# Adding x to the projected attention on TensorE with an identity product

## The chip, the cores and the metric

The kernel runs on one core of one Trainium2 chip. The metric is device time in microseconds, of the median of several executions. Engines are named TensorE (PE; its weight loads are PEld), VectorE (DVE), ScalarE (ACT), GpSimd (POOL) and SyncE (SP).

## The reference

The input x has shape (8, 384, 64, 64), in float32. Two layers are applied, each as x plus a function of the group-normed x. The first is a channel attention, the second a selective scan over four directions. All convolutions of 1x1 are matrix products over the channels.

```python
# layer 0: channel attention
q = _dwconv3x3(_conv1x1(x, wq), dwq)      # k and v likewise
q, k, v = (split(q), split(k), split(v))  # 8 heads of 48 channels
q = _l2norm(q)
k = _l2norm(k)
attn = softmax(einsum('bhcn,bhdn->bhcd', q, k) * temperature)
out = einsum('bhcd,bhdn->bhcn', attn, v)
out = _conv1x1(out, wproj)
...
x = x + _L0_conv_ref(_gn(x), ...)
x = x + _L1_conv_ref(_gn(x), ...)         # its group norm needs statistics of the new x
```

## The kernel before, in words

The eight images are worked on one after the other. Each goes through `channel_attention` and then through `selective_scan`. Channels lie on partitions, in three tiles of 128 (index m or j); pixels lie along the free dimension, 4096 per image, in eight chunks of 512 (index c). Everything is float32. The image x stays in SBUF from its load until the scan has used it.

`channel_attention` makes k, then q, then v with the same helper `conv` (L203 to L244). For a tile m and a stretch of rows y0 to y1, TensorE makes the 1x1 convolution in chunks of eight image rows (L219, into a PSUM tile "pc"), ScalarE copies each chunk out with its bias into the SBUF tile "pre" (L224) and starts the depthwise sum with the centre tap (L228), and VectorE adds the other eight taps (L240). The tile "pre" has two buffers.

The last part of the attention makes v and projects it. The product of the attention matrix and the projection has been folded into one matrix mT (L337, L340). The rows come in three stretches, 0 to 32, 32 to 48 and 48 to 64 (L359), each for the three tiles m. Where a stretch ends, its last row of pre-activation is kept (L367, "edge") and put in front of the next stretch's "pre" (L213), so that x itself is not needed there again.

`project_out(m, c)` (L346 to L356) handles one block of 128 channels by 512 pixels. TensorE makes three products over the three tiles of v into one PSUM tile (L349). VectorE adds it to x in place (L354) and takes the statistics for the next group norm from the result (L355). SP stores the new x to DRAM (L356), where the finish step of the following image's attention reads it.

Blocks are queued in `todo` as their rows of v become known, and are issued after later convolutions, six at a time and only for m above 0 (L368 to L370). A stretch of 32 rows gives twelve blocks, a stretch of 16 gives six. So 18 of an image's 24 blocks are issued inside the loop, in three groups of six: after the conv of tile 1 and of tile 2 in the stretch 32 to 48, and after that of tile 1 in the stretch 48 to 64. The last six are issued after the loop (L374).

The PSUM tiles of `conv` and of `project_out` come from one pool, `ps_c`, under one tag with three buffers (L168), so a block and a conv chunk wait for each other's buffers.

From the second image on, the loop also carries the finish of the image before (L371, `finish_part`, L856 to L878): SP loads a part of the scan's result and of the stored x, ScalarE normalizes it (L865), TensorE turns it (L872), ScalarE applies the gelu (L873), VectorE adds x (L877) and SP stores it. Two parts follow each convolution.

In this part the order of the instructions on each engine is chosen by a scheduler that works from priorities and estimated durations when the program is built; nothing in it is pinned. Each engine then works through its queue in that order. In the scan, by contrast, the order is written out by hand (`pin`), and the change doesn't touch it. After the attention, the scan starts with the group norm's factors (L114 to L140) and normalizes x in place (L417, L422).

Of the kernel before, what the change touches and what calls it, by code (L numbers as in the profile page):

```python
# [17 lines left out]
NJ = C // P  # L18
H = W = 64
L = H * W  # L20
CH = 512
# [53 lines left out]
def tile_channel_attention_then_selective_scan(ctx: ExitStack, tc: tile.TileContext, a: dict):  # L75
    nc = tc.nc
# [7 lines left out]
    ident = const.tile([P, P], F32, name="ident")  # L84
# [13 lines left out]
    for name in ("dt_bias", "Ds", "ln_w", "ln_b", "temp"):  # L98
        t = const.tile(list(a[name].shape), F32, name=name)
# [43 lines left out]
    def load_x(b):  # L143

        xs = []
        for j in range(NJ):
            t = big.tile([P, L], F32, tag="x", bufs=NJ, name=f"x{b}_{j}")
            for h in range(2):
                nc.sync.dma_start(t[:, bass.ts(h, L // 2)], x_d[b, j, :, bass.ts(h, L // 2)])
            xs.append(t)  # L150
        stats = big.tile([P, NJ, NCH, nc.vector.BN_STATS_DIM], F32, tag="st0", name=f"st0{b}")
        return xs, stats
# [6 lines left out]
    def channel_attention(b, x, stats, before):  # L159
# [5 lines left out]
        with ExitStack() as st:  # L165
# [122 lines left out]
            for m in range(NJ):  # L288
# [7 lines left out]
                for t4 in range(NT // 4):  # L296
                    qT = work.tile([P, 4, P], F32, tag="qT", name=f"qT{b}{m}_{t4}")
                    to_tokens(acc, t4, qT, f"q{b}{m}")
                    for i in range(4):
                        t = 4 * t4 + i  # L300
                        nc.tensor.matmul(
                            pa[:, :wd], lhsT=qT[:, i, :], rhs=kT[:, t, lo:hi],
                            start=t == 0, stop=t == NT - 1,
# [18 lines left out]
            if before is not None:  # L322
                scale, shift = token_norm(b, wp, work, before[2])

                def emit(i):
                    t = work.tile([P, L], F32, tag="acc", name=f"fin{b}_{i}")
                    room = [t[:, n * FT * NJ : (n + 1) * FT * NJ] for n in range(3)]
                    finish_part(*before, i, scale, shift, room, ps_t, "pt")
# [3 lines left out]
            for j in range(NJ):  # L332
                pm = ps_a.tile([P, CH], F32, tag="pa", name=f"pmt{b}{j}")
                src = [i for i in range(NJ) if _overlaps(i, j)]
                for i in src:
                    nc.tensor.matmul(
                        pm[:, :C], lhsT=attn[:, i, bass.ts(j, P)], rhs=wj[:, i, :],  # L337
                        start=i == src[0], stop=i == src[-1],
# [4 lines left out]
            x1_d = dram.tile([NJ, P, L], F32, tag="x1d", bufs=2, name=f"x1d{b}")  # L343
            stats1 = big.tile([P, NJ, NCH, nc.vector.BN_STATS_DIM], F32, tag="st1", name=f"st1{b}")

            def project_out(m, c):  # L346
                pc = ps_c.tile([P, CH], F32, tag="pc", name=f"pp{b}{m}_{c}")
                for j in range(NJ):
                    nc.tensor.matmul(  # L349
                        pc, lhsT=mT[:, j, bass.ts(m, P)], rhs=v[:, j, bass.ts(c, CH)],  # L350
                        start=j == 0, stop=j == NJ - 1,
                    )
                s = x[m][:, bass.ts(c, CH)]
                nc.vector.tensor_add(s, s, pc)  # L354
                nc.vector.bn_stats(stats1[:, m, c, :], s)  # L355
                nc.sync.dma_start(x1_d[m, :, bass.ts(c, CH)], s)  # L356


# [1 line left out]
            todo, left, edges = [], list(range(L // FT)) if emit else [], {}  # L360
            for y0, y1 in zip(parts, parts[1:]):
                for m in range(NJ):
                    pre = conv("v", wv, bv, m, y0, y1, v[:, m, y0 * W : y1 * W], edges.get(m))
                    if y1 < H:
                        edges[m] = work.tile([P, W], F32, tag="edge", bufs=4, name=f"edge{b}{m}_{y1}")
                        o = (y1 - 1 - max(0, y0 - 1)) * W
                        nc.scalar.copy(edges[m], pre[:, o : o + W])  # L367
                    if m > 0:  # L368
                        for _ in range(min(len(todo), 6)):
                            project_out(*todo.pop(0))  # L370
                    for _ in range(min(len(left), 2)):  # L371
                        emit(left.pop(0))
                todo += [(m, c) for c in range(y0 * W // CH, y1 * W // CH) for m in range(NJ)]
            for t in todo:  # L374
                project_out(*t)
        return x, x1_d, stats1

    def selective_scan(b, x1, stats1):
# [514 lines left out]
    x, before = load_x(0), None  # L893
    x_stats(*x, [(j, c) for j in range(NJ) for c in range(NCH)])
    for b in range(B):
        x1, x1_d, stats1 = channel_attention(b, *x, before)
        y_d, x = selective_scan(b, x1, stats1)
        before = (b, x1_d, y_d)
# [50 lines left out]
```

## Time and profile before

| | us |
|---|---|
| median of 3 runs | 20936.09 (20930.49 to 20946.7) |
| the profiled execution | 20922.88 |
| its span, first to last instruction | 20921.1 |
| VectorE busy / TensorE busy | 19312.5 / 19277.1 |
| ScalarE busy / GpSimd busy | 18022.9 / 15437.3 |
| products of `project_out` (L349), 1152 records | 556.1 |
| adds of x (L354), 192 | 129.7, one 687 ns |
| statistics of the new x (L355), 192 | 130.9, one 694 ns |
| mean granted TensorE clock | 0.966 of full speed |

The span is slightly shorter than the time of the same execution, since the time also holds what lies around the first and the last instruction. A line such as L349 is the number of the line in the kernel. "out<-in" names the tile that an instruction writes and those that it reads. In a timeline the first two columns are the start and the length of a merged run of instructions, "x36" says how many there are, and the bracket at the end gives how long the engine stood idle before and who ended that. A table of stretches has, for each stretch, its length and then the busy time of each engine with the count of instructions, the granted TensorE clock, the busy share of the DMA engines and GB/s.

### The profile page before, as it was taken

Reading aid. Unit: us, or ns where it says so; the run is one execution under the profiler, and the core shown is the slowest. Engines: PE = TensorE matmul, PEld = TensorE weight load, DVE = VectorE, ACT = ScalarE, POOL = GpSimd, SP = SyncE. Lnnn points to the kernel's source line nnn. Section 1 sums busy time; section 2 is a strip of 40 time slices with the busy share of each in tenths; the row PEclk is TensorE's granted clock in tenths of the full one; section 3 lists DMA queues with packets and bytes.
Section 4 is the critical chain, followed back from the end, with each engine's and each line's share of the span. In section 5 each row is a group of like instructions: output and inputs, shape, how many; then the busy total and the mean of one; then the engine's idle time right before and its main releaser. Section 6 shows DMA issues by size and latency. Waiting matters only on the chain. (4 is left out here: it accounts for less than half of the span.)

```text
span 20921.1 us, 319325 instructions
## 1 busy us (share of the span) xinstructions
PE 19277.1 (92%) x118256; PEld 10697.2 (51%) x118256; DVE 19312.5 (92%) x17310; ACT 18022.9 (86%) x32267; POOL 15437.3 (74%) x6918
## 2 busy tenths in 40 slices
PE   7999989999899998999989999899998999989998
PEld 4555445555455554555445555455544555445554
DVE  8999989999899988999889998899988999889998
ACT  3999949999599985999859998599985999859998
POOL 0999809998199981999719997199971999729997
PEclk8999989999899998999989999899998999989999
DMA  1222322223223232222322223223232232322223
GB/s 41 78 91 93 95 75 81 91 92 96 73 81 91 92 99 70 81 91 92 102 69 81 91 92 102 70 79 91 93 99 71 81 92 92 97 71 82 91 91 116
DMA packets 953163, 1807.95 MB, mean 86 GB/s; under 512 B 125904, under 2 KB 646352, under 8 KB 945456
## 3 DMA queue, kind: packets, MB, share of 16 engines
q1 hardware_dynamic: 950736, 1787.40, 27.0%
q8 instruction: 932, 15.27, 0.3%
q14 instruction: 631, 5.17, 0.1%
q10 hardware_dynamic: 864, 0.12, 0.0%
HBM read 1468.39 MB, written 318.77 MB: 85 GB/s over the span
## 5 line engine op out<-in xcount | busy, mean ns | idle before, releaser
L553 POOL TENSOR_TENSOR db<-w,B 128x1536 f32<-128x1536 f32 x4088 | 14134.1, 3464 | 639.9 <-DVE h L565 283.9
L565 DVE TENSOR_TENSOR_SCAN h<-da,ca,db 128x512 f32<-128x512 f32 x10752 | 13085.7, 1268 | 627.2 <-ACT da L544 316.6
L599 ACT ACTIVATE hc<-pt,ct 128x384 f32<-128x384 f32 x15128 | 8517.5, 579 | 452.1 <-PE pt L587 353.0
L544 ACT ACTIVATE da<-dt,neg_a 128x512 f32<-128x512 f32 x12288 | 8508.7, 696 | 183.3 <-DVE h L565 148.2
L587 PE MATMUL pt<-ident,h 128*128 128x128 f32 x49152 | 8097.9, 288 | 582.9 <-ACT hc L599 412.3
L587 PEld LDWEIGHTS pt<-ident,h 128*128 128x128 f32 x49152 | 5150.5, 141 | 5243.1 <-ACT hc L599 2648.5
L622 PE MATMUL py<-hc,pair 128*64 128x384 f32 x24576 | 5347.7, 514 | 9.2 <-DVE ys L673 9.2
L402 POOL MEMSET wdt<- 128x1536 f32 x8 | 11.0, 1378 | 3614.3 <-DMA x1d<-x 3614.3
L628 PE MATMUL py<-hc,pair 128*64 128x128 f32 x24576 | 2114.2, 281 | 0.0
L565 DVE TENSOR_TENSOR_SCAN h<-da,db 128x512 f32<-128x512 f32 x1536 | 1814.0, 1232 | 160.6 <-ACT da L544 98.9
L622 PEld LDWEIGHTS py<-hc,pair 128*64 128x64 f32 x24576 | 1218.5, 135 | 1020.3 <-issue 950.9
L628 PEld LDWEIGHTS py<-hc,pair 128*64 128x64 f32 x24576 | 1568.5, 137 | 208.9 <-issue 130.4
L451 PE MATMUL px<-x,wx 128*44 128x128 f32 x6144 | 1482.4, 339 | 35.3 <-ACT x L417 29.1
L451 PEld LDWEIGHTS px<-x,wx 128*44 128x44 f32 x6144 | 649.1, 122 | 816.7 <-issue 750.9
L528 POOL TENSOR_TENSOR w<-x,dt 128x512 f32<-128x512 f32 x744 | 1056.0, 1419 | 0.0
L579 POOL COPY ca<-h 128x6 f32<-128x6 f32 x1792 | 339.3, 189 | 943.7 <-DVE h L565 940.4
L510 PE MATMUL pd<-xd,wdt 128*128 128x512 f32 x1536 | 781.5, 618 | 73.0 <-ACT hc L599 60.6
L601 DVE TENSOR_SCALAR hc<-pt,ct 128x384 f32<-128x384 f32 x1256 | 736.2, 603 | 54.8 <-PE pt L587 25.4
L349 PE MATMUL pp<-v,mT 128*128 128x512 f32 x1152 | 556.1, 637 | 121.8 <-DVE v L240 57.3
L520 ACT ACTIVATE dt<-pd,dt_bias 128x512 f32<-128x512 f32 x768 | 474.6, 685 | 21.3 <-PE pd L510 17.7
L510 PEld LDWEIGHTS pd<-xd,wdt 128*128 128x128 f32 x1536 | 274.6, 192 | 387.0 <-issue 187.1
L349 PEld LDWEIGHTS pp<-v,mT 128*128 128x128 f32 x1152 | 229.5, 205 | 402.0 <-issue 314.4
(315 smaller groups left out, 11723.8 us busy)
## 6 DMA issues: line engine op xcount, KB each, us to landing
B<-bcd SPq DMA_DIRECT2D x2048, 512.0 KB
yd<-ys SPq DMA_DIRECT2D x128, 576.0 KB
ys<-yd SPq DMA_DIRECT2D x256, 288.0 KB
yd<-ys SPq DMA_DIRECT2D x256, 288.0 KB
x<-in_x SPq DMA_DIRECT2D x48, 1024.0 KB
x1d<-x SPq DMA_DIRECT2D x192, 256.0 KB
fy<-yd SPq DMA_DIRECT2D x128, 384.0 KB
fin<-yd SPq DMA_DIRECT2D x112, 384.0 KB
```

The lines of the kernel that those rows point to most:

```text
L349: nc.tensor.matmul(pc, lhsT=mT[:, j, bass.ts(m, P)], rhs=v[:, j, bass.ts(c, CH)], start=j == 0, stop=j == NJ - 1,)
L451: pin(nc.tensor.matmul(split(pxs[s][:XR, :])[:, part, :], lhsT=wx[:, j, k, :], rhs=view(x1[j], k, c)[:, part, :], start=i == 0, stop=i == ...
L510: pin(nc.tensor.matmul(pds[j], lhsT=wdt[:, k, bass.ts(j, P)], rhs=xds[s], start=True, stop=True))
L528: pin(eng.tensor_mul(split(ws[s][:, j, :]), view(x1[j], k, c), split(dts[s][:, j, :])))
L544: pin(nc.scalar.activation(t, dts[s][:, j, :], AF.Exp, scale=neg_a[:, j, k, n : n + 1]))
L553: pin(eng.tensor_mul(t, ws[g // NP], bts[g][:, v : v + 1, :].broadcast_to([P, NJ, CH])))
L565: pin(nc.vector.tensor_tensor_scan(h, da, db, 0.0 if start else carries[s - 1][:, j, n : n + 1], ALU.mult, ALU.add,))
L587: pin(nc.tensor.transpose(t[:, bass.ts(j, P)], h2s[g][:, j, bass.ts(q, HP), :].rearrange("p l v -> p (l v)"), ident))
L599: pin(eng.activation(out, src, AF.Copy, scale=scale))
L601: pin(eng.tensor_scalar_mul(out, src, scale))
L622: pin(nc.tensor.matmul(py[f * HP : (f + 1) * HP, lb, :C], lhsT=pair, rhs=hc[:, f, :], **flags))
L628: pin(nc.tensor.matmul(py[f * HP : (f + 1) * HP, j, C:], lhsT=pair, rhs=hc[:, f, bass.ts(j, P)], **flags,))
```

## The change

For the 18 blocks that are issued inside the loop, `project_out` now begins the PSUM sum with a product of the identity matrix and the chunk of x, so that the finished PSUM tile holds the new x. VectorE takes the statistics from PSUM; it no longer adds. ScalarE copies the tile from PSUM over the chunk of x, and the store follows that copy. For the six blocks after the loop the code is as before. The identity matrix `ident` was in SBUF already.

```diff
-            def project_out(m, c):
+            def project_out(m, c, end):
+
+                s = x[m][:, bass.ts(c, CH)]
                 pc = ps_c.tile([P, CH], F32, tag="pc", name=f"pp{b}{m}_{c}")
+                if not end:
+                    nc.tensor.matmul(pc, lhsT=ident, rhs=s, start=True, stop=False)
                 for j in range(NJ):
                     nc.tensor.matmul(
                         pc, lhsT=mT[:, j, bass.ts(m, P)], rhs=v[:, j, bass.ts(c, CH)],
-                        start=j == 0, stop=j == NJ - 1,
+                        start=end and j == 0, stop=j == NJ - 1,
                     )
-                s = x[m][:, bass.ts(c, CH)]
-                nc.vector.tensor_add(s, s, pc)
-                nc.vector.bn_stats(stats1[:, m, c, :], s)
+                if end:
+                    nc.vector.tensor_add(s, s, pc)
+                    nc.vector.bn_stats(stats1[:, m, c, :], s)
+                else:
+                    nc.vector.bn_stats(stats1[:, m, c, :], pc)
+                    nc.scalar.copy(s, pc)
                 nc.sync.dma_start(x1_d[m, :, bass.ts(c, CH)], s)
...
                         for _ in range(min(len(todo), 6)):
-                            project_out(*todo.pop(0))
+                            project_out(*todo.pop(0), False)
...
             for t in todo:
-                project_out(*t)
+                project_out(*t, True)
```

In the built program of the changed kernel the scheduler has also moved a few neighbours on TensorE: the transposes of a finish part (L872), of which the first used to stand before the last block of a group, stand after it. On ScalarE the copies stand between the finish activations. The wait that is written into each copy is for VectorE, whose statistics read the same PSUM tile.

## The prediction

> **What bounds the kernel now.** I started with the page's busy times, to see that no one engine rules everything.
>
> ```profile
> PE 19277.1 (92%) x118256; PEld 10697.2 (51%) x118256; DVE 19312.5 (92%) x17310; ACT 18022.9 (86%) x32267; POOL 15437.3 (74%) x6918
> L349 PE MATMUL pp<-v,mT 128*128 128x512 f32 x1152 | 556.1, 637 | 121.8 <-DVE v L240 57.3 <-ACT pre0v L224 15.5 <-DVE x L354 9.0
> ```
>
> TensorE and VectorE tie at 92%, over 2,100 us of scan per image that the change doesn't touch. The row L349 counts 1152 records for 8 images x 24 blocks x 3 products = 576 products, so a fp32 product is two records ("passes"). What the change is worth is read where these blocks run: the last 110 us of each attention. I asked for the busy time in five stretches of the second image (2890 us to 3062 us).
>
> ```profile
> core 0: us, PE busy (x) PEld busy (x) DVE busy (x) ACT busy (x) POOL busy (x), PEclk, DMA share, GB/s
> 2955.00:2982.00 27.00, 26.91 (x70) 12.57 (x71) 23.77 (x29) 10.60 (x21) 0.00 (x0) 0.91 0.56 183
> 2982.00:3004.40 22.40, 22.40 (x62) 10.44 (x61) 18.50 (x22) 8.44 (x15) 0.00 (x0) 1.00 0.52 177
> 3004.40:3036.40 32.00, 30.25 (x85) 13.31 (x84) 29.79 (x32) 16.18 (x27) 0.00 (x0) 1.00 0.53 181
> 3036.40:3062.00 25.60, 17.31 (x41) 7.77 (x40) 19.39 (x23) 0.00 (x0) 1.83 (x3) 0.80 0.28 93
> ```
>
> Call the first three A, B, C; each holds one group of six blocks of the 18 that change. In A and B TensorE is busy throughout and VectorE is not; in C both nearly are. The fourth is the tail, whose blocks keep their code. The same stretches of images 2 and 7 have the same figures within 0.3 us. Then the timeline, VectorE and TensorE, for who waits.
>
> ```profile
> 2981.90 1.27 DVE L240 SCALAR_TENSOR_TENSOR v<-pre1v,dwv,v 128x1008 f32<-128x1008 f32 x1 [3.23 <-ACT v L228]
> 3004.43 7.74 DVE L240 SCALAR_TENSOR_TENSOR v<-pre1v,dwv,v 128x1008 f32<-128x1008 f32 x6 [3.54 <-ACT v L228]
> 3017.77 0.68 DVE L354 TENSOR_TENSOR x<-x,pp 128x512 f32<-128x512 f32 x1
> 3036.41 10.23 DVE L240 SCALAR_TENSOR_TENSOR v<-pre1v,dwv,v 128x1008 f32<-128x1008 f32 x8 [1.59 <-ACT v L228]
> ```
>
> ```profile
> 2954.77 15.70 PE L349 MATMUL pp<-v,mT 128*128 128x512 f32 x30 [5.94 <-ACT pre1v L224]
> 2980.32 15.67 PE L349 MATMUL pp<-v,mT 128*128 128x512 f32 x36
> 3018.50 2.84 PE L349 MATMUL pp<-v,mT 128*128 128x512 f32 x6 [0.66 <-DVE x L354]
> 3029.05 5.42 PE L219 MATMUL pc1v<-x,wv 128*128 128x512 f32 x12 [0.38 <-DVE x L354]
> ```
>
> ```profile
> 3002.53 0.69 ACT L224 ACTIVATE pre1v<-pc1v,bias1v 128x512 f32<-128x512 f32 x1 [1.89 <-PE pc1v L219]
> 3003.25 1.15 ACT L228 ACTIVATE v<-pre1v,dwv 128x1024 f32<-128x1024 f32 x1
> ```
>
> At the end of each group VectorE stands still until ScalarE's L228, which waits for L224, which waits for the conv product L219, which stands behind the group's products in TensorE's queue. So the chain through A and B is: 36 passes of L349, the next conv's passes, L224, L228, first tap. VectorE has 3.23 and 3.54 us to spare.
>
> [...] Here a pass goes every 0.43 us (36 passes in 15.67 us), a product in 0.86: the trace decides. [...] after 5.94 us of idle the weight loads of A's first passes stand 0.86 us apart. [...] no row of before has two readers of a block, but the built order shows each copy waiting for VectorE, so statistics and copy of a block are in series. [...] the trace has 687 for the add.
>
> **The change, part by part.** 18 blocks x 8 images = 144 changed blocks.
>
> Removed: 144 adds on VectorE. One lasts 687 ns, but neighbours overlap: in the timeline the next instruction starts 0.60 us after an add. 6 x 0.60 = 3.6 us a group, 86 us in all. In A and B VectorE is not on the chain, so this only lengthens its idle time; in C part of it counts.
>
> Statistics from PSUM: before reads SBUF in 694 ns. [...] the add that reads PSUM takes 687[...]; I take 0. VectorE's slack covers it[...].
>
> Added: 144 identity products, two passes of 0.4275 us each: 0.86 x 6 = 5.1 us a group, 123 us in all. Their weight loads lie beside passes (PEld is half busy). In the built order the identity product stands first in each block. Could it fill the 5.94 us ahead of A? Those wait for PSUM: all three buffers hold the conv of the stretch before, until L224 frees them, and the identity product needs such a buffer too. So it starts where the first pass starts today, and follows on the chain.
>
> Added: 144 copies on ScalarE at about 0.69 us (L224, the same shape out of PSUM, 687 ns): 4.1 us a group, where ScalarE is busy 38 to 51%. It carries a wait for VectorE, and behind it in ScalarE's queue stand finish activations (L865, L873), L213 and later L224. A buffer now comes free after product, statistics and copy rather than after the add. Walking A: blocks end every 3.4 us, so a buffer is needed again 6.9 us after its block's end; statistics (up to 2 us behind a tap) and copy (0.7, at most 1.5 behind a pair of finish activations) take under 4.5. No stall inside a group. At its end there is one: the transposes of the finish parts (L872), formerly slipped in before the sixth block, stand after it in the built order, alternating with the conv's products, and each pair waits for a gelu L873 on ScalarE, one of them behind the sixth copy. Their 1.3 us of work is in both kernels; the ping-pong exposes about 0.2 us in A, 0.7 in B, by laying the orders out with 0.56 us per gelu and 0.86 per product.
>
> Stores of x1 (L356, now L363) wait for the copy instead of the add, 1 us later; behind them in SP's queue stand the finish loads, needed by ScalarE after the next conv, which is itself 5 us later. POOL's memset waits for the tail's stores, which are unchanged. Nothing.
>
> Sums for images 1 to 7. A: 5.1 + 0.2 = 5.3. B: 5.1 + 0.7 = 5.8. C: TensorE reaches the fourth block when VectorE frees the first buffer, 13.3 us into C (3017.77). In after the first three blocks need 2.6 us more and end about 16.0 us in; the first statistics come one tap later than the add did (14.5), the copy is done by 15.8; the fourth block starts at 16.0 (today 14.1, 3018.50). Three blocks of 3.43 end at 26.3; conv, transposes and ping-pong of 7.3 end at 33.6; L224 and L228 as today (1.9) give the first tap at 35.5. Today it is 32.0: +3.5, lower than 5.1 because the 0.66 and 0.38 us waits for the add and part of VectorE's own delay go. Tail: the same eight taps and six blocks, 0. Together 14.6 us an image, 102 for seven.
>
> The first image has no finish parts:
>
> ```profile
> 382.60 1.27 DVE L240 SCALAR_TENSOR_TENSOR v<-pre0v,dwv,v 128x1008 f32<-128x1008 f32 x1 [5.56 <-ACT v L228]
> 403.77 14.60 DVE L240 SCALAR_TENSOR_TENSOR v<-pre0v,dwv,v 128x1008 f32<-128x1008 f32 x12 [4.39 <-ACT v L228]
> 419.02 10.37 PE L349 MATMUL pp<-v,mT 128*128 128x512 f32 x18 [4.31 <-DVE x L354]
> ```
>
> A and B: 5.1 each. In C TensorE stands 4.31 us for the first add, so 2.6 us of identity products vanish there; the last 18 passes took 10.37 us at a cold clock, 24 warm ones take 10.3; the copy adds 0.7: +0.8. Image: 11. Sum 102 + 11 = 113 us. The profiled execution took 20922.88 us (span 20921.1), giving 21036; it lies 13 us under the median of the runs, 20936.09, to which I add: 21049.
>
> **The rivals.** *The add was the bound* (faster): if VectorE's queue, not TensorE's, released the next group, 86 us go: 20850. For it: 92% busy, 29.79 of 32.00 us in C. Against: 3.2 and 3.5 us of idle in A and B. It decides if TensorE's extra 5.1 us a group finds cover, in all three groups, that the trace doesn't show. *C gains instead of losing*: A and B +5.1 each, C -3.6 because VectorE's queue rules it: 6.6 x 8 = 53, 20989. For it: the waits for L354 in C. Against: TensorE has 1.75 us of idle in C, against 5.1 of new work. *The copies hold the buffers*: a copy stuck behind a finish activation that waits for its load (up to 3.1 us there today) stalls TensorE some 2 us a group beyond 5.1: 7.1 x 3 x 8 = 170, 21106. For it: three buffers for conv and blocks alike. Against: the 6.9 us of room.
>
> **Numbers.** Forecast 0.74, C gains 0.10, copies hold 0.10, add was the bound 0.06. The forecast's own spread: with no ping-pong (C then 2.6) 12.8 an image, 7 x 12.8 + 11 = 101, 21037; with 0.7 us more per group 16.7 an image, 128, 21064. The range reaches down to the C case and up towards the copies: 20985 to 21095. Within 0.2% (42 us, about what this measurement tells from no change) falls half of the C case: faster 0.06, same 0.06, slower 0.88.
>
> **What would show it.** Right: 144 x 2 records of an identity product 0.43 us apart; VectorE's idle before the first tap after A and B up from 3.2 and 3.5 to 12 or 13; A and B about 32 and 28 us long with TensorE still full; the tail unchanged. Wrong: TensorE idle inside a group waiting for ScalarE's copy (copies hold), or A and B no longer than today with VectorE full (add was the bound).

## The result, and the profile after

The changed kernel takes 21044.18 us (median of five runs, 21037.56 to 21047.34), the kernel before 20938.42 (20930.49 to 20946.7). The ratio is 1.005, with a 95% interval of 1.0036 to 1.0065: 106 us slower. The forecast was 21049.

The profiled execution of after is its median run, with a span of 21042.3 us, while the profiled execution of before lay 15 us below its median; so the spans differ by 121 us, the medians by 106. First its busy times, from the page.

```profile
PE 19407.8 (92%) x118544; PEld 10759.8 (51%) x118544; DVE 19240.7 (91%) x17166; ACT 18108.8 (86%) x32411; POOL 15436.0 (73%) x6918
```

TensorE has 131 us more work than before, ScalarE 86 more, VectorE 72 less. The groups of after say in what (count, busy time, mean ns of one, then the idle time just ahead of them and who ended most of it):

```profile
L353 PE MATMUL pp<-v,mT 128*128 128x512 f32 x1152 | 560.0, 629 | 57.4 <-DVE v L240 57.4
L351 PE MATMUL pp<-x,ident 128*128 128x512 f32 x288 | 157.0, 628 | 59.4 <-ACT pre0v L224 15.5 <-ACT pre1v L224 6.1 <-ACT pre5v L224 6.1
L361 DVE BATCH_NORM_STATS2 st<-pp 128x6 f32<-128x512 f32 x144 | 100.1, 695 | 108.4 <-PE pp L353 107.7
L362 ACT COPY x<-pp 128x512 f32<-128x512 f32 x144 | 83.5, 581 | 172.6 <-DVE st L361 172.6
```

L351 is the identity product, 288 records for 144 products. The old row of products (L349, now L353) waited 57.3 us for VectorE's last tap and still does: that is the tail. What is new is 107.7 us in which VectorE, about to take statistics (L361), stands idle for TensorE's products. The time saved on VectorE has become waiting.

Then the stretches A, B, C and tail of the second image, bounded as before by the first product of the group and the first taps after each group (columns as in the prediction's table):

```profile
2974.74:3006.89 32.15, 32.15 (x82) 15.04 (x83) 21.09 (x22) 13.82 (x27) 0.00 (x0) 0.92 0.48 160
3006.89:3034.67 27.78, 27.78 (x74) 12.73 (x73) 15.72 (x17) 11.74 (x21) 0.00 (x0) 1.00 0.42 141
3034.67:3069.52 34.85, 34.29 (x97) 15.64 (x96) 26.59 (x26) 19.17 (x33) 0.00 (x0) 1.00 0.51 171
3069.52:3094.91 25.39, 17.51 (x40) 7.73 (x38) 19.02 (x23) 0.00 (x0) 1.29 (x1) 0.80 0.23 78
```

With the same bounds A was 27.13 us and is 32.15, B was 22.53 and is 27.78, and TensorE is busy for every us of both. In C TensorE now is busy for 34.29 of 34.85 us, where it had 1.75 us to spare in 32.00. The tail is as it was. VectorE's timeline shows how it waits at the end of A, and ahead of the three first taps:

```profile
2994.85 0.70 DVE L361 BATCH_NORM_STATS2 st<-pp 128x6 f32<-128x512 f32 x1 [2.12 <-PE pp L353]
2998.29 0.70 DVE L361 BATCH_NORM_STATS2 st<-pp 128x6 f32<-128x512 f32 x1 [2.73 <-PE pp L353]
...
3006.89 2.59 DVE L240 SCALAR_TENSOR_TENSOR v<-pre1v,dwv,v 128x1008 f32<-128x1008 f32 x2 [3.74 <-ACT v L228]
...
3034.67 5.20 DVE L240 SCALAR_TENSOR_TENSOR v<-pre1v,dwv,v 128x1008 f32<-128x1008 f32 x4 [3.64 <-ACT v L228]
...
3069.52 10.23 DVE L240 SCALAR_TENSOR_TENSOR v<-pre1v,dwv,v 128x1008 f32<-128x1008 f32 x8 [3.65 <-ACT v L228]
```

The wait for L228 ahead of the tap has hardly grown in A and B (3.23 to 3.74, 3.54 to 3.64). A reader who looked at those rows alone would find no loss. The rest of the idle time lies a few lines earlier: VectorE finishes its taps and waits block by block (2.12, 2.73) for the statistics of the last blocks, and then for the finish adds. Over the whole of A it is 32.15 - 21.09 = 11.1 us idle. TensorE's timeline has the other side:

```profile
2974.74 2.08 PE L351 MATMUL pp<-x,ident 128*128 128x512 f32 x2 [6.10 <-ACT pre1v L224]
...
2994.65 1.02 PE L351 MATMUL pp<-x,ident 128*128 128x512 f32 x2
2995.51 2.74 PE L353 MATMUL pp<-v,mT 128*128 128x512 f32 x6
2998.09 0.60 PE L879 MATMUL pz<-ident,fin 128*128 128x128 f32 x4
```

A block now takes 2998.09 - 2994.65 = 3.44 us, of which the identity product is 2995.51 - 2994.65 = 0.86. It stands behind the same wait for L224 (6.10 us, once 5.94), so it fills none of it.

All figures below are put together in one table. "v to end" is the time from the first conv product of v to the last statistics aggregate of the attention (L114), read from the timelines: 198.0 us before in the first image, 204.7 on average in the other seven. It holds everything that the change touches. The last column sums it over eight images. The medians are taken against runs of before made beside them (20938.42 for after, 20926.1 for the next four rows, 20934.03 for the four below these, 20924.32 for the last two).

| kernel | median against before, us | ratio (95%) | v to end, first image | images 2 to 8 | sum against before |
|---|---|---|---|---|---|
| before | 0 | | 198.0 | 204.7 | 0 |
| after | +105.8 | 1.005 (1.0036 to 1.0065) | 211.6 | 218.2 | +108 |
| product of zeros, add stays | +82.8 | 1.0039 (1.0025 to 1.0053) | 209.0 | 217.3 | +99 |
| no product | -4.5 | 0.9998 (0.999 to 1.0006) | 198.5 | 205.9 | +8 |
| copies on VectorE | +110.0 | 1.0053 (1.004 to 1.0065) | 212.1 | 218.3 | +109 |
| two products | +187.6 | 1.009 (1.0076 to 1.0104) | 222.6 | 232.7 | +220 |
| third group only | +17.9 | 1.0009 (1.0001 to 1.0017) | 201.3 | 206.8 | +18 |
| blocks spread 4, 4, 4, 2, 2, 2 | -45.1 | 0.9978 (0.997 to 0.9987) | 187.4 | 201.7 | -32 |
| conv ahead | -61.9 | 0.9971 (0.996 to 0.9982) | 190.0 | 199.5 | -44 |
| conv ahead, with product | +40.4 | 1.0019 (1.0012 to 1.0027) | 193.6 | 213.5 | +57 |
| three per conv | -96.5 | 0.9954 (0.9942 to 0.9967) | 183.0 | 194.9 | -84 |
| three per conv, with product | -35.2 | 0.9983 (0.9977 to 0.999) | 192.4 | 201.8 | -26 |

The two differences disagree by up to 32 us, for two reasons. The last column rests on one profiled execution of each kernel, and that of before is 1 to 15 us faster than the medians above. And the scan, whose code no kernel changes, isn't equally long in all of them: over eight images it is 12 us longer in after than in before, and 33 us shorter with two products. In after these two nearly cancel. The section on the hardware comes back to the scan.

### The profile page after: what moved, and what is told of

Its sections match the earlier page's. It is cut to its first block, busy times and chain, and to the rows that moved or that the text cites. A ratio compares the mean times of both kernels' runs of the same rounds, so it can differ in the third digit from the quotient of the medians.

```text
span 21042.3 us, 319886 instructions
## 1 busy us (share of the span) xinstructions
PE 19407.8 (92%) x118544; PEld 10759.8 (51%) x118544; DVE 19240.7 (91%) x17166; ACT 18108.8 (86%) x32411; POOL 15436.0 (73%) x6918
## 5 line engine op out<-in xcount | busy, mean ns | idle before, releaser
L353 PE MATMUL pp<-v,mT 128*128 128x512 f32 x1152 | 560.0, 629 | 57.4 <-DVE v L240 57.4
L353 PEld LDWEIGHTS pp<-v,mT 128*128 128x128 f32 x1152 | 232.9, 204 | 356.8 <-issue 346.9
```

What stands on the lines that cost most here:

```text
L353: nc.tensor.matmul(pc, lhsT=mT[:, j, bass.ts(m, P)], rhs=v[:, j, bass.ts(c, CH)], start=end and j == 0, stop=j == NJ - 1,)
```

## The experiments

My theory: TensorE's queue ahead of the next conv sets the pace of these stretches, so each identity product costs its own duration there. First rival: the copies and the statistics from PSUM hold the block's buffer and cost the time. Second rival: VectorE's adds counted, so that taking them away gives something back.

**A product alone.** Before, with one more product in each of the 18 blocks, whose weights are all zero; the add stays on VectorE. The making of the tile of zeros and the passing of `end` are left out here.

```diff
+                if not end:
+                    nc.tensor.matmul(pc, lhsT=zero, rhs=s, start=True, stop=False)
                 for j in range(NJ):
...
-                        start=j == 0, stop=j == NJ - 1,
+                        start=end and j == 0, stop=j == NJ - 1,
```

> The kernel before, with one product more in each of the 18 blocks of an image: zero weights times the chunk of x, which adds nothing. The add and the statistics stay on VectorE, nothing is copied by ScalarE. If TensorE's queue in front of the next conv sets the time (my theory), A and B grow by 5.1 us each and C by about 3, as in the changed kernel: 100 to 120 us over before, although no other engine has a new instruction. If ScalarE's copies and their hold on the PSUM buffers cost the time, this one costs 0 to 40. If VectorE were the bound, about 0.

Measured +82.8 us. A, B and C of the later images are 31.8, 27.7 and 34.6 us long (means), within 0.4 of after. The product alone makes nearly the whole loss inside the attention (+99 of +108). The median misses the expected 100 to 120, mostly because the scan is 12 us shorter in this run than in before.

**Everything but the product.** After without the identity product. x is left out of the sum for the 18 blocks; the statistics from PSUM and the copies stay.

```diff
-                if not end:
-                    nc.tensor.matmul(pc, lhsT=ident, rhs=s, start=True, stop=False)
...
-                        start=end and j == 0, stop=j == NJ - 1,
+                        start=j == 0, stop=j == NJ - 1,
```

> The changed kernel without the identity product: x is left out of the sum, so the statistics and the copy take the bare projection. VectorE still has no add, ScalarE still has 144 copies behind the statistics. My theory: the chain through A and B is back to 36 passes, C may gain up to 3 us or lose 1, so -25 to +15 us against before. If the copies cost the time: +60 to +110. If the add had been a bound, -86.

Measured -4.5 us, no difference that can be told. In A and B taking the adds from VectorE gives nothing, and the copies with statistics from PSUM cost nothing: they are 27.0 and 22.6 us long, as before. Only C is longer, 34.1 for 31.8, since the fourth block waits for a buffer that comes free after statistics and copy. TensorE's timeline in C of the second image shows it (L351 is the row of products and L360 the copy in this kernel):

```profile
3024.78 9.69 PE L351 MATMUL pp<-v,mT 128*128 128x512 f32 x18 [1.13 <-ACT x L360]
```

The tail gives 1.1 us of it back. So the second rival falls, and the first falls in A and B. In C it doesn't quite: the copy's hold alone lengthens C by 2.3 us and the product alone by 2.8, while both together make 3.2. There the two waits lie beside each other, and either would have cost most of it.

**The copies on VectorE.** After, with VectorE copying in place of ScalarE.

```diff
-                    nc.scalar.copy(s, pc)
+                    nc.vector.tensor_copy(s, pc)
```

> The changed kernel, but VectorE copies the block out of PSUM after its statistics; ScalarE has no copies, VectorE has as much to do as before. My theory: VectorE has over 3.6 us to spare in A and B, so they stay as in the changed kernel, C may lose 1 or 2 us an image: +105 to +125 us over before. If ScalarE's copies cost the time, +0 to +60.

Measured +110.0, as expected: which engine copies doesn't matter. VectorE pays for the copies out of its waiting.

**A second product.** After, with a product of zero weights behind the identity product.

```diff
                     nc.tensor.matmul(pc, lhsT=ident, rhs=s, start=True, stop=False)
+                    nc.tensor.matmul(pc, lhsT=zero, rhs=s, start=False, stop=False)
```

> The changed kernel with a second product in each of the 18 blocks, zero weights times the chunk of x. My theory: another 5.1 us in each of the three groups of eight images, now in C too, since TensorE has no idle time left there: 123 us over the changed kernel, +225 to +235 over before. If the first product's cost came from something else than its length on TensorE (its wait for x or for a buffer), the second adds much less: under +150 over before.

Measured +187.6, 82 more than after. In the attention the second product costs what the theory says: A +5.0, B +5.2, C +4.9 over after, and C no longer has any cover. The sum is 220 for 108. But the scan is 33 us shorter than in before, and so the median misses the expected 225 to 235.

**The third group only.** After, with the change confined to C.

```diff
-                            project_out(*todo.pop(0), False)
+                            project_out(*todo.pop(0), y1 < H)
```

> The kernel after, with the identity product, the statistics from PSUM and the copy in the third group alone; the groups of A and B are as before. Theory (each group pays on its own chain, and C less than A and B because its waits for the add go): 20 to 30 us more than before, C 3.0 us longer in each image and A and B unchanged. Rival (a third of the whole): 35 us more. Rival (in C, where VectorE is busy for 29.8 of 32.0 us, the removed adds count): 0 to 20 us less than before.

Measured +17.9, a little under the expected 20 to 30; the interval reaches from +2 to +36. VectorE's first taps in the second image:

```profile
2992.82 1.27 DVE L240 SCALAR_TENSOR_TENSOR v<-pre1v,dwv,v 128x1008 f32<-128x1008 f32 x1 [3.23 <-ACT v L228]
...
3015.35 7.74 DVE L240 SCALAR_TENSOR_TENSOR v<-pre1v,dwv,v 128x1008 f32<-128x1008 f32 x6 [3.54 <-ACT v L228]
...
3049.98 5.20 DVE L240 SCALAR_TENSOR_TENSOR v<-pre1v,dwv,v 128x1008 f32<-128x1008 f32 x4 [3.64 <-ACT v L228]
```

The first two waits are those of before to the hundredth; only the third is that of after. B is 3015.35 - 2992.82 = 22.53 us long as before, C 34.63. C is 3.0 longer on average and the tail 0.6 shorter. So the groups pay one by one, and C pays less than A or B. The rival that the removed adds would shorten C falls.

**The same blocks, laid out otherwise.** If the pace is set by what TensorE has in its queue around a conv, the layout should matter more than the add. Before, with the blocks dealt out more evenly:

```diff
-                    if m > 0:
-                        for _ in range(min(len(todo), 6)):
-                            project_out(*todo.pop(0))
+                    for _ in range(min(len(todo), 4 if y1 < H else 2)):
+                        project_out(*todo.pop(0))
```

> The kernel before, with the 18 blocks dealt out four to each conv of the stretch 32 to 48 and two to each conv of the last stretch, instead of six to three of these convs. Theory (what costs is the TensorE work queued in one piece ahead of a conv that VectorE waits for): with four blocks instead of six the chain is 5.1 us shorter than VectorE's taps in most places, so that most of the 8.3 us an image that VectorE stands idle before its first taps goes: 20 to 60 us less than before. Rival (TensorE's total work between 2955 and 3036 us of the profiled span is the limit, wherever it is queued): within 15 us of before.

Measured -45.1, inside the theory's range: with the same work on both engines the kernel is faster, so TensorE's total work was not the limit. And before, with the blocks' PSUM tiles out of another pool:

```diff
-                pc = ps_c.tile([P, CH], F32, tag="pc", name=f"pp{b}{m}_{c}")
+                pc = ps_a.tile([P, CH], F32, tag="pa", name=f"pp{b}{m}_{c}")
```

> The kernel before, with the blocks' PSUM tiles taken from the pool of the other products (two buffers) instead of sharing the three buffers of the conv chunks; the built order then puts the next conv ahead of most of the group in A and lets a block slip between later ones. Theory (a group ahead of the conv is the chain): VectorE's idle time before the first taps, 3.2 us after A and 3.5 us after B in each image, goes at least in A: 20 to 60 us less than before. Rival (TensorE's total work is the limit): within 15 us of before. Second rival (with two buffers the blocks wait for VectorE's add and hold up the conv behind them): 20 to 80 us more.

Measured -61.9, just beyond the expected 20 to 60. TensorE's timeline shows the new order: two of a block's products, and straight behind them the next conv.

```profile
2950.33 3.42 PE L349 MATMUL pp<-v,mT 128*128 128x512 f32 x4 [5.02 <-DVE v L240]
2953.58 5.31 PE L219 MATMUL pc1v<-x,wv 128*128 128x512 f32 x12
```

VectorE's timeline has no idle time at all from 2925 to 2990 us, a stretch that holds this group. The second rival, two buffers too few, did not come. This edit changes the order and also gives the blocks buffers of their own; how much each is worth wasn't tried apart.

**The product where the conv goes ahead.** After, with the same other pool.

> The kernel after, with the blocks' PSUM tiles taken from the pool of the other products, as in the run before. Theory: where the conv goes ahead of the group, the identity products are no longer on the chain and only fill TensorE's queue beside VectorE's taps; in A most of the 5 us goes, in B and C part of it: 20 to 80 us more than before instead of 106. Rival (TensorE's total work is the limit): 95 to 120 us more than before, as in after.

Measured +40.4. That is in my range, but not for my reason. The right comparison is the run before it: with the product it takes 102 us more than without, as much as in the old layout. Only in the first image, which has no finish parts, did the product find cover (193.6 against 190.0 us). In the others it cost 14.0 us an image. The built order isn't that of the run without it: ten blocks now stand ahead of the conv that follows, from the first of these lines to the second, with nothing but a few transposes between them:

```profile
2963.87 1.08 PE L351 MATMUL pp<-x,ident 128*128 128x512 f32 x2
...
2999.61 1.02 PE L219 MATMUL pc1v<-x,wv 128*128 128x512 f32 x2
```

"On the chain or not" was too simple a question. It is a question of balance: how long each engine works for one conv and the blocks that go with it.

**The balance, tested.** Three blocks behind each of the six convs, with the other pool, without and with the product.

```diff
-                    if m > 0:
-                        for _ in range(min(len(todo), 6)):
-                            project_out(*todo.pop(0))
+                    for _ in range(min(len(todo), 3)):
+                        project_out(*todo.pop(0))
```

> The kernel before, with three blocks behind each of the six convs and the blocks' PSUM tiles from the pool of the other products. Balance per conv, from durations of the traces: VectorE eight taps 10.2 + three blocks 3 x 1.2 + two finish adds 1.2 = 15.0 us; TensorE conv 5.2 + three blocks 3 x 2.57 + transposes 1.3 = 14.2 us. Theory: VectorE no longer waits, 60 to 110 us less than before, at least as fast as the run with the conv ahead. Rival (the blocks' adds, now among the taps, hold up the buffers and cost what the balance gains): within 30 us of before.

Measured -96.5 us: the best version of all, and faster than both kernels. VectorE's timeline in the last stretch, where one conv's eight taps start with each of these lines:

```profile
2996.67 1.26 DVE L240 SCALAR_TENSOR_TENSOR v<-pre1v,dwv,v 128x1008 f32<-128x1008 f32 x1
...
3011.24 1.26 DVE L240 SCALAR_TENSOR_TENSOR v<-pre1v,dwv,v 128x1008 f32<-128x1008 f32 x1
```

No bracket: in this round VectorE doesn't wait. It lasts 14.57 us, and the two before it 15.06 and 14.77, where 15.0 were worked out for VectorE. With the product:

> The kernel after, with the same two edits. Balance per conv: VectorE 10.2 + 3 x 0.6 + 1.2 = 13.2 us; TensorE 5.2 + 3 x 3.43 + 1.3 = 16.8 us. Theory (the identity product moves work from an engine that is not above the other to one that then is): TensorE sets the pace of each conv, 16.8 against 15.0, so 1.8 us x 6 x 8 = 86 us more than the run without the product, between 50 and 115. Rival (only the piling up of six blocks ahead of a conv made the identity product dear): 0 to 30 us more than the run without it, or less.

Measured -35.2, that is 61 us more than without the product. The same view:

```profile
3013.36 2.59 DVE L240 SCALAR_TENSOR_TENSOR v<-pre1v,dwv,v 128x1008 f32<-128x1008 f32 x2 [3.52 <-ACT v L228]
...
3030.26 2.59 DVE L240 SCALAR_TENSOR_TENSOR v<-pre1v,dwv,v 128x1008 f32<-128x1008 f32 x2 [3.52 <-ACT v L228]
```

A round lasts 16.90 us, where 16.8 were worked out for TensorE, and the wait of 3.52 us is back. Round by round, from first tap to first tap, the product adds -2.8, +4.9, +2.6, +1.8 and +2.3 us (means of images 2 to 8), and the last round together with the tail is 2.1 shorter. So an image is only 6.9 us longer (9.4 in the first): the first round and the tail give a part back, for a reason that wasn't tried. So the product costs something even in the best layout found. The rival, that only the piling up made it dear, falls. The two pairs that share the other pool differ in the layout alone, and there piling up raises the product's price from 61 to 102 us.

## Why the prediction was right

- **What bounds it.** Right. TensorE is full in A and B and stays so. A product of zeros does nearly all of the damage, and taking the adds away does nothing.
- **The identity products, 5.1 us a group.** Right: 0.86 us each. On the average of seven images A is 4.9 longer and B 5.25.
- **The ping-pong of transposes and gelus, 0.2 and 0.7 us.** Not found. TensorE has no idle time at the end of A or B. The terms 5.3 and 5.8 were about half a us too large.
- **C, +3.5.** Measured +3.2. The steps hold: the fourth block starts 15.7 us into C (16.0 was worked out), the first tap comes at 34.85 (35.5). The copy that frees its buffer ends at the same 15.7 (15.8), so here TensorE and the copy tie.
- **The tail, 0.** Measured +0.15.
- **Statistics from PSUM, 0.** 695 ns against 694.
- **The adds, 86 us off VectorE and none off the end.** Right in what counts; the busy time fell by 72 only. In part that is because statistics that start after idle time add 0.70 us to the busy time, and 0.61 where they follow an instruction at once and overlap its end.
- **The copies, 0.69 us.** Mis-sized: 586 ns (median). I took L224, an ACTIVATE with a bias, which takes 687 for the same shape out of PSUM, 101 more than the copy. It changed nothing, as ScalarE has room (busy for 19.17 of 34.85 us in C).
- **The copies don't hold the buffers.** Right for after, though narrowly in C: the run without the product shows that they do hold TensorE up where it comes earlier. Who waited for L362 in all of after (us, times):

```profile
  PEld pp L351: 9.6, 13
  PE pp L351: 2.4, 1
```

The one wait of the products is in the first image. In the other places only a weight load waited, and the product behind it shows no wait of its own.

- **The idle time of 12 or 13 us "before the first tap".** Half right. The amount is there, 11.1 us in A and 12.1 in B, but in pieces: in A 4.9 us before the statistics, 2.2 before the finish adds and 3.7 before the tap, in B 6.0, 2.3 and 3.6. I had not asked what stands in VectorE's queue ahead of the tap: the last blocks' statistics, which wait for the same products, and the finish adds behind them.
- **The first image's C, +0.8.** Mis-sized: +2.5. I held that the last three blocks, with 24 passes at the full clock, take 10.3 us, as 18 did in before at a mean granted clock of 0.77. TensorE's timeline there:

```profile
432.93 1.30 PE L351 MATMUL pp<-x,ident 128*128 128x512 f32 x2 [2.37 <-ACT x L362]
434.03 4.30 PE L353 MATMUL pp<-v,mT 128*128 128x512 f32 x6
438.17 1.02 PE L351 MATMUL pp<-x,ident 128*128 128x512 f32 x2
```

The wait fell from 4.31 to 2.37 us as worked out, but the first block took 438.17 - 432.93 = 5.24 us in place of 3.44. The clock granted over this block was 0.67: it fell here too, after about half the wait. In the run with two products there was no wait, the clock was 1.00 throughout and this C took 36.1 us, only 0.9 longer than after.

The sum for images 2 to 8 was 102 and came to 94, that for the first 11 and came to 13.5: 113 against 108. The misses had opposite signs, so that the total is nearer than some of its parts, and that is luck. So is part of the 5 us between forecast and median: the five runs of before alone lie up to 16 us apart. The scan, put at nothing, took 12 us more in after's profile than in before's.

## What to carry to other kernels

Work that two equally busy engines share is worth moving only if the one that takes it has idle time in that stretch. Make the balance for one round of the stage, the sum of each engine's durations, and not from the shares of the whole span. Here a fp32 product of 0.86 us took the place of an add that costs 0.60 us of an engine that was waiting anyway. The same balance showed where the time was: three blocks behind each conv, instead of six behind three of them, and buffers of their own gave 97 us. When looking for a stall, sum an engine's idle time over the stretch: the wait ahead of the instruction that one suspects may stay as it was while others grow beside it.

## What the runs showed of the hardware that was not expected

**A slow block after a short idle time.** In the first image of after, 2.37 us of idle on TensorE, from 430.56 to 432.93 us, were followed by a slow block: the granted clock is 1.00 from 432.93 to 433.75 us and 0.50 from there to 437.16 us, for 3.41 us. That the idle time was the cause was not shown.

**How fast the scan starts goes with the moment at which the clock falls.** The 14 small products of the group norm (first line of each pair) and the first scan projections (second line) in the second image, after and with two products:

```profile
3097.00 3.14 PE L134 MATMUL pv<-var,avg 128*128 128x1 f32 x14 [0.84 <-DVE var L129]
3103.76 5.35 PE L458 MATMUL px<-x,wx 128*44 128x128 f32 x24 [3.61 <-ACT x L424]
```

```profile
3117.97 1.83 PE L136 MATMUL pv<-var,avg 128*128 128x1 f32 x14 [0.84 <-DVE var L131]
3123.40 4.20 PE L461 MATMUL px<-x,wx 128*44 128x128 f32 x24 [3.61 <-ACT x L427]
```

The instructions and the waits are the same, the durations 1.3 and 1.15 us shorter. The granted clock over the first line's products is 0.50 in after and 0.90 with two products. In after it falls to half 0.86 us ahead of them, with two products 1.47 us behind their start. Their duration goes with that one moment in all 96 starts of a scan that the twelve traces hold: 3.14 or 3.15 us where the clock fell ahead of the first of these products (42 starts), 1.72 to 1.75 us where it fell 1.5 us or more behind it (18), and between these where it fell in between (36).

How busy the attention was doesn't decide it. With two products, the busiest, they take 1.72 to 1.83 us in all eight images; but without the product, where TensorE has the same blocks to do as in before, they take 1.75 to 2.27, and before itself has 1.72 in its first image and 3.14 or 3.15 in the others. With the blocks spread out they take 1.72 in three images and 3.14 or 3.15 in five, with the same instructions. In the traces of before and after the recorded changes of the clock lie whole multiples of 3.41 us apart, and in their 16 starts the fall comes 2.2 to 5.3 us after the attention's last product, a spread of about one such step. From these numbers I estimate that it depends on where in this raster the attention happens to end; that was not shown, and what could move it on purpose was not tried.

Over an image's scan the run with two products is 5.4 us faster than after (2161.5 against 2166.9, means of seven). These two rows explain 2.5 us of it; the rest I have not located. So up to some 30 us of a kernel's difference here can come from code that it doesn't touch.
